# A two-layer decoder on one Trainium2 core: the gate norms of batches 0 and 1 tied to a place in VectorE's order

## The chip, the cores and the metric

The kernel runs on one core of a Trainium2 chip. The metric is the device time of one execution in microseconds (us), lower is better. Five engines work side by side, each through its own queue in order: TensorE (PE, with its weight loads shown as PEld), VectorE (DVE), ScalarE (ACT), GpSimd (POOL) and SyncE (SP), which issues most of the transfers (DMAs).

## What is computed

Six sublayers, each with a layer norm in front and a residual addition behind, act on `x` of 4 batches x 512 tokens x 256 channels, all in float32:

```python
x = x + _L0_attn_ref(_layernorm(x), ...)    # gated scan over time, 16 heads of 32
x = x + _L0_xattn_ref(_layernorm(x), ctx)   # cross attention, 16 heads of 16
x = x + _L0_ffn_ref(_layernorm(x), ...)     # 8 experts + 4 zero experts, top 2
x = x + _L1_attn_ref(_layernorm(x), ...)    # log-space recurrence
x = x + _L1_xattn_ref(_layernorm(x), ctx)   # ternary weights, int8 steps
x = x + _L1_ffn_ref(_layernorm(x), ...)     # 8 experts, top 2
```

The change lies where the second sublayer ends and the third begins. The third takes `layernorm(x)`, scores each token against 12 experts (`logits = x @ gate_w.T + bias`), takes the two best and mixes their outputs:

```python
logits = jnp.einsum('btd,ed->bte', x, gate_w) + expert_bias
topk_logits, topk_idx = jax.lax.top_k(logits, TOP_K)
topk_w = jax.nn.softmax(topk_logits, axis=-1)
```

## The kernel before

Layer 0's two mixers are one function, `l0_mixers`. Its core is a loop over 16 units `u` (and one more turn to end): unit `u` is batch `b = u // 4` and head group `m = u % 4`, four heads of the cross attention. A unit has eight steps `n`. Step `n` issues `exponents(u, ...)` (L919): PE multiplies keys by queries into a score tile of PSUM (two buffers), DVE takes the negated maxima into `tops` (L927), ACT takes the exponentials into `e` (L930). After it come the jobs that were appended with `after(n, job, ...)` for this step, in the order of appending.

In the steps of unit `u` the unit before is ended: `least(u - 1)` at step 1 finds the least maximum, `weigh(u - 1)` at step 2 forms the weights: PE spreads the value, DVE subtracts `tops` from it into `behind` (L950), ACT exponentiates it, POOL multiplies the values by it into `weighed` (L953). `gather_values(u - 1, j)` at steps 3 to 6 multiplies the weighted values by `e` on PE (L965, "av").

Other work is spread over the steps by hand: the first sublayer's work for later batches (`absorb`, `tokens` with the token norm, `turn_tokens`, `split` into q, `keep` and so on), `project` that adds the attention's output to `x` (L1060), `fold_piece` (products of the last sublayer's weights, from unit 11 on), and from unit 11 on the routing of the third sublayer by the class `Places`:

- `norm(b)` (L1497): a layer norm of a batch's four row tiles on DVE. `moments` (L173) issues four pairs of BATCH_NORM_STATS2 (L179) and BATCH_NORM_AGGREGATE (L180); `rstd` (L166) issues eleven small instructions one after another (L169, L160, then L162, L163, L164 three times); four TENSOR_SCALAR at L1504 write the normed tile `gh_b`. The small tiles of the norm have one buffer each.
- `transpose(b, c)` (L1508): PE turns four blocks of `gh_b` (L738), ACT copies them into `ght_b` (L1511), for the channel halves c = 0 and 1.
- `score(b, ...)` (L1513): 16 small matmuls and one DVE addition (L1523) give the logits; `pick` and `rank` find the two experts and the rows; `put` writes the rows by indirect transfers (L1575).

Two things set the order of the work. PE's instructions and the loads and stores on SP's queue are pinned in the order in which they are written (`pinned`, `turn` and `move` call `tc.keep_in_program_order`). The order on DVE, ACT and POOL is made when the kernel is built: what is written earlier comes first among what is ready by the planner's reckoning, so that an instruction whose inputs are there early may be put ahead of others that are written before it. `tc.add_manual_dep` with class `NoSync` adds an order between two instructions of one engine without a semaphore; the kernel uses it for `blank` and `put`, which are put behind the last `weighed` product on POOL.

The jobs of units 11 and 12 that the change concerns are these:

```python
if u == 11:
    after(1, g.norm, 0)
    for c in range(DC):
        after(4 + c, g.transpose, 0, c)
    after(5, g.norm, 1)
    after(6, g.score, 0, (0, 1))
elif u == 12:
    for c in range(DC):
        after(1 + c, g.transpose, 1, c)
    after(3, g.score, 1, (0, 1))
    after(4, g.pick, (0, 1))
```

Norms 2 and 3 follow in unit 13 and behind the loop.

Of the kernel before, what the change touches and what calls it, by code (L numbers as in the profile page):

```python
# [18 lines left out]
P = 128  # L19
# [4 lines left out]
QT = T // P  # L24
# [17 lines left out]
class Kernel:  # L42
# [127 lines left out]
        self.inverse_root(y, half, u)  # L170
        return y

    def moments(self, srcs, pool):  # L173

        nc, n = self.nc, len(srcs)
        st = pool.tile([P, n, nc.vector.BN_STATS_DIM], F32, tag="ln_st", name="ln_st")
        mv = pool.tile([P, n, nc.vector.BN_AGGR_DIM], F32, tag="ln_mv", name="ln_mv")
        for i, s in enumerate(srcs):
            nc.vector.bn_stats(st[:, i, :], s)  # L179
            nc.vector.bn_aggr(mv[:, i, :], st[:, i, :])  # L180
        return mv

# [358 lines left out]
def l0_mixers(k):  # L541
# [21 lines left out]
    with ExitStack() as es:  # L563
# [159 lines left out]


        normal, mixed, raw, sums_of, squares, factors, gated, outs = {}, {}, {}, {}, {}, {}, {}, {}
        weighing, near_of, factor_of = {}, {}, {}

        def normalize(b):
            normal[b] = k.layer_norm(b)
# [214 lines left out]
        def weigh(u):  # L944

            b, m = divmod(u, 4)
            ps, diag = lows[u]
            pinned(ps[:, P : P + 4], [(k.ones[:4, :], diag)])
            behind = sp.tile([P, QT, 4], F32, tag="behind", name=f"behind_{u}")
            nc.vector.tensor_sub(behind, ps[:, None, P : P + 4].to_broadcast([P, QT, 4]), k.tops[:, u])  # L950
            wt = weighed[u % 2]
            nc.scalar.activation(wt[:, :, :, 16], behind, AF.Exp)
            weighing[0] = nc.gpsimd.tensor_mul(  # L953
                wt[:, :, :, 0:16],
                vs[u],
                wt[:, :, :, 16:17].to_broadcast([P, QT, 4, 16]),
            )
# [232 lines left out]
        ps = bank("v_bias")  # L1190
# [25 lines left out]
        for u in range(units + 1):  # L1216
            b, m = divmod(u, 4)
            if m == 0 and b < NB:
                atts[b] = wk.tile([P, 4, T], F32, tag="att", name=f"att_{b}")

            then = {n: [] for n in range(8)}

            def after(n, f, *args):
                then[n].append((f, *args))

            if u + 1 < units:
                after(0, gather, u + 1)
                after(4, fetch_values, u + 1)
            if 0 < u < units:
                after(1, least, u - 1)  # L1230
                after(2, weigh, u - 1)
            if 2 <= u < 10:
                after(3, blank, u - 2)
            near_b, next_b, last_b = b + 1, b + 2, b + 3
            if u == FOLDING:

                mixers.close()
                k.fold_pool = ExitStack()
                k.fold_w = k.fold_pool.enter_context(tc.tile_pool(name="fold_w", bufs=2, side="right"))
                k.places = Places(  # L1240
                    k, k.fold_pool.enter_context(tc.tile_pool(name="places", bufs=1, side="right")),
                    move, bank, turn, pinned, new_ht,
                )
                after(7, fetch_fold, 0)
            elif u > FOLDING:
                if u < units:
                    for j, n in enumerate((0, 1, 2, 7)):
                        after(n, fold_piece, 4 * (u - FOLDING - 1) + j)
                g = k.places
                if u == 11:  # L1250
                    after(1, g.norm, 0)
                    for c in range(DC):
                        after(4 + c, g.transpose, 0, c)
                    after(5, g.norm, 1)
                    after(6, g.score, 0, (0, 1))
                elif u == 12:
                    for c in range(DC):
                        after(1 + c, g.transpose, 1, c)
                    after(3, g.score, 1, (0, 1))
                    after(4, g.pick, (0, 1))  # L1260
                    after(7, g.rank, (0, 1))
                elif u == 13:
                    for i in range(QT):
                        after(2 + i, project, 2, i)
                        after(3 + i, g.put, 0, i, weighing)
                    after(7, g.norm, 2)
                elif u == 14:
                    for c in range(DC):
                        after(1 + c, g.transpose, 2, c)
                    for i in range(QT):  # L1270
                        after(3 + i, g.put, 1, i, weighing)
                    after(3, g.score, 2, (2,))
                    after(3, g.pick, (2,))
                    after(6, g.rank, (2,))
                elif u == 15:
                    for i in range(QT):
                        after(3 + i, g.put, 2, i, weighing)
            if m == 0:
                if near_b < NB:
                    after(0, recall, near_b, 1)  # L1280
                    after(1, factor, near_b, 2)
                    after(3, recall, near_b, 2)
                    after(3, factor, near_b, 3)
                    after(5, recall, near_b, 3)
                    for j in range(3):
                        after(3 + 2 * j, emit, near_b, j)
            elif m == 1:
                if 1 <= b < NB - 1:
                    after(0, invert, b - 1)
                    after(2, give_back, b - 1)  # L1290
                    after(4, spread, b - 1, 0)
                    after(6, spread, b - 1, 1)
                if near_b < NB:
                    after(1, emit, near_b, 3)
                    after(2, absorb, near_b)
                    after(4, tokens, near_b)
                if next_b < NB:
                    for j in range(4):
                        after(2 + j, measure, next_b, j)
                    for j in range(4):  # L1300
                        after(4 + j, total, next_b, j)
            elif m == 2:
                if near_b < NB:
                    for c in range(DC):
                        after(1 + c, turn_tokens, near_b, c)
                    for mc in range(2):
                        after(3 + mc, split, near_b, mc, "q")
                        after(5 + mc, keep, near_b, mc, "q")
                if next_b < NB:
                    after(0, scale, next_b)  # L1310
                    after(2, scale_near, next_b)
                    after(4, scale_far, next_b)
                if last_b < NB:
                    after(5, normalize, last_b)
                if 1 <= b < NB - 1:
                    for i in range(QT):
                        after(4 + i, project, b - 1, i)
            elif next_b < NB:
                for j in range(4):
                    after(j, gated_values, next_b, j)  # L1320
                after(1, factor, next_b, 0)
                after(3, factor, next_b, 1)
                after(4, recall, next_b, 0)
                if last_b < NB:
                    for c in range(DC):
                        after(5 + c, mix, last_b, c)
            if u == units:
                after(0, least, u - 1)
                after(0, share_sums, NB - 1, 2)
                after(0, weigh, u - 1)  # L1330
                after(0, share, NB - 1, 2)
                for j in range(QT):
                    after(0, gather_values, u - 1, j)
                for m in range(2):
                    after(0, project_early, NB - 1, m)
            elif u > FOLDING - 1:

                done = divmod(u - 2, 4)
                after(0, share_sums, *done)
                after(1, share, *done)  # L1340
            if 0 < u < units:
                for j in range(QT):
                    after(3 + j, gather_values, u - 1, j)
                if m == 0 and b < NB - 1:
                    after(7, collect, b - 1)
            for n in range(8):
                if u < units:
                    exponents(u, n // 4, n % 4)
                for f, *args in then[n]:
                    f(*args)  # L1350
# [104 lines left out]
class Places:  # L1455
# [38 lines left out]
        self.carry = self.start  # L1494
        self.h, self.ht, self.logits, self.picks = {}, {}, {}, {}

    def norm(self, b):  # L1497
        k = self.k
        h = self.h[b] = self.pool.tile([P, QT, D], F32, name=f"gh_{b}")
        srcs = [k.x[:, t, :] for t in range(NT)[k.tiles(b)]]  # L1500
        mv = k.moments(srcs, self.pool)
        r = k.rstd(mv[:, :, 1], QT, self.pool)
        for i, s in enumerate(srcs):
            k.nc.vector.tensor_scalar(  # L1504
# [817 lines left out]
```

## Time and profile before

| | us |
|---|---|
| five runs: median (lowest to highest) | 1273.62 (1270.16 to 1276.92) |
| the profiled execution, its own time | 1269.21 |
| its span, first to last instruction | 1267.5 |
| PE busy | 998.0 (79%) |
| DVE busy | 812.1 (64%) |
| ACT busy | 412.6 (33%) |
| POOL busy | 188.8 (15%) |
| mean granted TensorE clock | 0.883 |

The profile is of one execution. Times in it count from its first instruction. In a timeline a line gives the start, the time taken, the engine, the source line, the operation, what is written and read, the shapes and the count (xN, neighbours of one kind are merged); in brackets stands the idle time before it and what ended it. In a table by stretches each engine has its busy time and the number of its instructions; PEclk is the granted clock of TensorE, 1.00 being full. The ends of matmuls are modelled, so neighbouring matmuls can overlap in the list.

### The profile page before, as it was taken

How to read it: one execution, taken by the hardware profiler on the slowest of the kernel's cores; microseconds unless marked ns; L12 is line 12 of the kernel's file. 1: busy time of each engine (PE TensorE's matmuls, PEld its weight loads, DVE VectorE, ACT ScalarE, POOL GpSimd, SP SyncE). 2: the span in 40 equal slices, each digit the busy share in tenths (PEclk: the TensorE clock that was granted, in tenths of full speed). 3: DMA queues.
4: the chain of work that ended last, by engine and by line, in shares of the span. 5: the costliest groups of instructions: out<-in, count | busy, mean ns of one | idle time of the engine just before them, and what ended most of it. 6: DMA issues, size and time to landing. Idle time of an engine off the chain costs nothing.

```text
span 1267.5 us, 12057 instructions
## 1 busy us (share of the span) xinstructions
PE 998.0 (79%) x3868; PEld 560.0 (44%) x3868; DVE 812.1 (64%) x1991; ACT 412.6 (33%) x708; POOL 188.8 (15%) x225
## 2 busy tenths in 40 slices
PE   5879588688876999789789999337754887779997
PEld 1444233233332566447566677114432443254443
DVE  6676697887679768534356931346776555986564
ACT  4513355455443454320111421022222443820000
POOL 5431112213113002222000000630012100000000
PEclk9989787888976999898799999668886998879999
DMA  5385515343433645535456261310010010020000
GB/s 155 101 267 203 145 49 162 108 136 127 135 119 110 208 132 182 165 108 180 151 183 185 90 225 45 104 50 0 1 38 1 33 51 17 1 67 0 32 19 20
DMA packets 90779, 129.97 MB, mean 103 GB/s; under 512 B 20268, under 2 KB 61740, under 8 KB 90700
## 3 DMA queue, kind: packets, MB, share of 16 engines
q1 hardware_dynamic: 84544, 111.29, 27.9%
q0 software_dynamic: 6144, 17.83, 4.1%
q8 instruction: 33, 0.54, 0.2%
q14 instruction: 38, 0.31, 0.1%
q10 hardware_dynamic: 20, 0.00, 0.0%
HBM read 86.56 MB, written 42.53 MB: 102 GB/s over the span
## 4 chain that ended last, share of the span: by engine, by line
PE 28%; DVE 13%; DMA 3%; ACT 2%; issue 2%; another core or an unknown queue 2%; ACTq 2%; POOL 0%; SPq 0%; POOLq 0%; DVEq 0%
PE y L212 9%; PE ef L212 7%; PE bav L212 2%; PE down L212 2%; DVE hid_tops L1868 2%; PE bsc L212 2%; ACTq L205 1%; PE f L212 1%; PE bet L2090 1%; PE bf L212 1%; PE gate L212 1%; DVE state L1790 1%; DMA W_f1T_sb<-in_W_f1T 1%; DVE q_tmp L1857 1%
## 5 line engine op out<-in xcount | busy, mean ns | idle before, releaser
L930 ACT ACTIVATE e<-score,tops 128x512 f32<-128x512 f32 x256 | 161.6, 686 | 171.7 <-DVE tops L927 100.5
L927 DVE TENSOR_REDUCE tops<-score 128x2 f32<-128x1024 f32 x128 | 155.7, 1218 | 47.2 <-PE score L588 43.1
L212 PE MATMUL y<-folded_sb,fht 128*128 128x512 f32 x256 | 112.8, 601 | 0.0
L588 PE MATMUL score<-query,key 64*128 64x512 f32 x256 | 68.0, 533 | 24.8 <-ACT e L930 19.7
L2178 DVE SCALAR_TENSOR_TENSOR x_sb<-y,tt_w,x_sb 128x256 f32<-128x256 f32 x128 | 61.8, 483 | 38.3 <-PE y L212 35.0
L965 PE MATMUL av<-e,weighed 128*32 128x512 f32 x512 | 76.6, 638 | 5.7 <-POOL weighed L953 5.7
L212 PE MATMUL ef<-sw,eact 128*128 128x256 f32 x320 | 79.1, 385 | 2.4 <-DVE ey L1668 2.4
L212 PE MATMUL ef<-eht,sw 128*128 128x320 f32 x256 | 78.4, 448 | 1.3 <-ACT eact L1657 1.3
L212 PEld LDWEIGHTS y<-folded_sb,fht 128*128 128x128 f32 x256 | 48.9, 193 | 59.9 <-issue 59.9
L588 PEld LDWEIGHTS score<-query,key 64*128 64x128 f32 x256 | 25.2, 197 | 100.7 <-ACT e L930 50.8
L588 PE MATMUL fold<-w_outT,w_in 128*128 128x256 f32 x256 | 66.1, 411 | 0.0
L212 PEld LDWEIGHTS ef<-sw,eact 128*128 128x128 f32 x320 | 58.5, 193 | 12.8 <-DVE ey L1668 5.1
L588 PE MATMUL o<-o_wT_sb,qk 128*128 128x256 f32 x128 | 46.9, 530 | 20.4 <-DVE qk L826 20.4
L212 PE MATMUL down<-W_downT_sb,state 128*128 128x256 f32 x96 | 33.7, 502 | 31.8 <-DVE state L1790 13.6
L212 PEld LDWEIGHTS ef<-eht,sw 128*128 128x128 f32 x256 | 48.6, 196 | 18.7 <-ACT eact L1657 2.0
L588 PEld LDWEIGHTS fold<-w_outT,w_in 128*128 128x128 f32 x256 | 50.5, 204 | 9.6 <-issue 2.6
L1657 ACT ACTIVATE eact<-ef 128x640 f32<-128x640 f32 x32 | 22.3, 703 | 98.2 <-PE ef L212 98.2
L212 PE MATMUL f<-aht,W_fT_sb 128*128 128x512 f32 x96 | 47.3, 652 | 6.4 <-issue 6.0
L588 PEld LDWEIGHTS o<-o_wT_sb,qk 128*128 128x128 f32 x128 | 32.8, 268 | 34.0 <-DVE qk L826 23.7
L203 PE MATMUL turn<-ident,h 128*128 128x128 f32 x96 | 17.1, 328 | 38.2 <-DVE ln_u L162 20.5
L1638 DVE COPY eht<-eturn 128x256 f32<-128x256 f32 x40 | 16.8, 420 | 43.7 <-PE eturn L1637 43.4
L1740 POOL DMA_INDIRECT got<-table,rows x32 | 30.8, 963 | 86.0 <-DVE neg_b L1732 76.6
(389 smaller groups left out, 1806.3 us busy)
## 6 DMA issues: line engine op xcount, KB each, us to landing
table<-zeros POOLq DMA_DIRECT2D x8, 1152.0 KB
factors<-far SPq DMA_DIRECT2D x64, 128.0 KB
key<-far_k SPq DMA_DIRECT2D x16, 512.0 KB
query<-far_q SPq DMA_DIRECT2D x16, 512.0 KB
w_in<-in_w_in SPq DMA_DIRECT2D x16, 512.0 KB
w_outT<-in_w_outT SPq DMA_DIRECT2D x16, 512.0 KB
rows<-table SPq DMA_DIRECT2D x8, 640.0 KB
table<-ey SPq DMA_DIRECT2D x8, 640.0 KB
```

Of the source, the lines that this page charges most:

```text
L203: nc.tensor.transpose(ps[:, i * P : (i + 1) * P], h[:, i, c * P : (c + 1) * P], self.ident)
L205: nc.scalar.copy(dst(c), ps)
L212: self.nc.tensor.matmul(out, lhs_t, rhs, start=(i == 0), stop=(i == len(pairs) - 1))
L588: nc.tensor.matmul(out, lhs_t, rhs, start=start and i == 0, stop=stop and i == len(pairs) - 1)
L927: nc.vector.tensor_reduce(top, ps, AX.X, ALU.max, negate=True)
L930: nc.scalar.activation(e[:, i, :], ps[:, i, :], AF.Exp, bias=top[:, i : i + 1])
L965: nc.tensor.matmul(avs[u][32 * h : 32 * h + 32, :], weighed[u % 2][:, j, h, :], es_of[u, h // 2, j][:, h % 2, :], start=(j == 0), stop=(j ...
L1638: nc.vector.tensor_copy(ht[:, :, i * P : (i + 1) * P], ps)
L1657: nc.scalar.activation(act[:, f, :].rearrange("p (j t) -> p j t", j=2), ps[:, :, :half], AF.Silu)
L1740: nc.gpsimd.indirect_dma_start(out=got[t, which], out_offset=None, in_=k.table, in_offset=bass.IndirectOffsetOnAxis(ap=k.rows[:, which, t ...
L1868: k.nc.vector.tensor_reduce(dst, src, AX.X, ALU.max, apply_absolute_value=True)
L2178: nc.vector.scalar_tensor_tensor(xt, ps[:, e, :], w[:, i, e4 + e : e4 + e + 1], xt, ALU.mult, ALU.add)
```

## The change

`moments` and `Places.norm` take an optional `behind`. Where it is given, each of the four BATCH_NORM_STATS2 gets a `NoSync` order behind the instruction that it holds. `weigh` keeps its DVE subtraction (`behind`, L950) in `weights[0]`. In unit 11 gate norms 0 and 1 are given `weights`: at both places it holds the subtraction of `weigh(10)`, which is issued in step 2 of unit 11. Norm 0 goes from step 1 to step 2, its two turns from steps 4 and 5 to 5 and 6, norm 1 from step 5 to 6 and the score of batch 0 from step 6 to 7. Everything else, norms 2 and 3 and the jobs of unit 12 too, is as it was.

```diff
-    def moments(self, srcs, pool):
+    def moments(self, srcs, pool, behind=None):
...
-            nc.vector.bn_stats(st[:, i, :], s)
+            stats = nc.vector.bn_stats(st[:, i, :], s)
+            if behind:
+                self.tc.add_manual_dep(
+                    stats.ins,
+                    behind[0].ins.name,
+                    mybir.DependencyInfo(mybir.DependencyClass.NoSync, mybir.DependencyReason.DATA),
+                    reason="behind a unit's weights",
+                )
             nc.vector.bn_aggr(mv[:, i, :], st[:, i, :])
...
-        weighing, near_of, factor_of = {}, {}, {}
+        weighing, weights, near_of, factor_of = {}, {}, {}, {}
...
-            nc.vector.tensor_sub(behind, ps[:, None, P : P + 4].to_broadcast([P, QT, 4]), k.tops[:, u])
+            weights[0] = nc.vector.tensor_sub(behind, ps[:, None, P : P + 4].to_broadcast([P, QT, 4]), k.tops[:, u])
...
                 if u == 11:
-                    after(1, g.norm, 0)
+                    after(2, g.norm, 0, weights)
                     for c in range(DC):
-                        after(4 + c, g.transpose, 0, c)
-                    after(5, g.norm, 1)
-                    after(6, g.score, 0, (0, 1))
+                        after(5 + c, g.transpose, 0, c)
+                    after(6, g.norm, 1, weights)
+                    after(7, g.score, 0, (0, 1))
...
-    def norm(self, b):
+    def norm(self, b, behind=None):
...
-        mv = k.moments(srcs, self.pool)
+        mv = k.moments(srcs, self.pool, behind)
```

## The prediction, made before the changed kernel was run

> **What bounds the kernel now.** I began with the page: PE is busy 79% of the span, DVE (VectorE) 64%, and the late part of the chain of waits lies behind the attention units, so a saving inside a unit counts only if it moves the unit's end. The 16 units are told apart in the list of DVE instructions by their eight "tops" reductions (L927). The first "tops" of units 9 to 13 start at 371.8, 393.6, 429.5, 450.9 and 472.5 us: unit 10 takes 35.9 us, unit 9 takes 21.8, unit 11 takes 21.4, unit 12 takes 21.6. Then the busy time by stretch, one row for each of units 10 and 11 (columns: length; PE, weight loads, DVE, ACT, POOL busy with counts; granted clock; DMA):
>
> ```profile
> core 0: us, PE busy (x) PEld busy (x) DVE busy (x) ACT busy (x) POOL busy (x), PEclk, DMA share, GB/s
> 393.60:429.50 35.90, 26.73 (x108) 13.72 (x108) 28.96 (x77) 13.08 (x22) 6.08 (x8) 0.72 0.40 127
> 429.50:450.90 21.40, 20.32 (x124) 12.95 (x125) 15.36 (x38) 11.56 (x21) 0.64 (x1) 1.00 0.44 141
> ```
>
> In unit 11 PE is the bound (20.32 of 21.40) and DVE has 6 us of air. Unit 10 is mixed, so I read its first 20 us in the timelines, DVE first:
>
> ```profile
> 401.93 2.20 DVE L190 TENSOR_SCALAR h<-x_sb,ln_mv,ln_y 128x256 f32<-128x256 f32 x4
> 404.05 0.68 DVE L164 SCALAR_TENSOR_TENSOR ln_y<-ln_u,ln_y 128x4 f32<-128x4 f32 x1
> 404.76 1.20 DVE L162 TENSOR_TENSOR ln_u<-ln_y 128x4 f32<-128x4 f32 x1
> ...
> 408.49 1.38 DVE L1504 TENSOR_SCALAR gh<-x_sb,ln_mv,ln_y 128x256 f32<-128x256 f32 x4
> 409.79 0.68 DVE L1036 TENSOR_TENSOR att<-att,share 128x512 f32<-128x512 f32 x1
> 410.39 1.21 DVE L927 TENSOR_REDUCE tops<-score 128x2 f32<-128x1024 f32 x1
> 411.52 0.16 DVE L950 TENSOR_TENSOR behind<-low,tops 128x16 f32<-128x16 f32 x1
> ```
>
> This is gate norm 0 (the L1504 rows write its "gh"). It is written in unit 11, step 1, but stands between the token norm of batch 3 ("h") and the third "tops" of unit 10. DVE has no gap over 0.1 us from 386.8 to 412.8. PE in the same stretch:
>
> ```profile
> 394.13 0.37 PE L937 MATMUL low<-ident,low 128*4 128x128 f32 x1
> 402.39 0.80 PE L738 MATMUL turn<-ident,h 128*128 128x128 f32 x2 [7.89 <-DVE h L190]
> ...
> 406.30 0.79 PE L588 MATMUL score<-query,key 64*128 64x512 f32 x2
> ...
> 409.30 3.78 PE L588 MATMUL q<-xht,w_q 128*128 128x512 f32 x4
> 413.85 1.07 PE L965 MATMUL av<-e,weighed 128*32 128x512 f32 x8 [0.77 <-POOL weighed L953]
> ```
>
> PE's order is pinned. It waits 7.89 us for "h", then works almost without a gap (0.26 us twice) until 413.1, at half clock (0.50 in the row 392.98 to 413.46), and waits 0.77 us for the weights. So gate norm 0's long tail at 404 to 410 delays the "tops", but PE is busy meanwhile: that is the point on which the forecast turns.
>
> **What is removed from units 9 and 10.** The undisturbed gate norm of the last batch runs from 571.40 to 576.75: 5.3 us (four L179/L180 pairs 1.75, eleven small steps at a pitch of 0.20 make 2.2, four L1504 1.4). Norm 0 costs more where it stands, since its L162 and L164 steps take up to 1.20 us while POOL runs two-input products (L1006): 5.7 us after "h", about 1.0 in front of "h" (one L179 at 400.57, L180s, L169, L160, L162, L163), 1.2 in unit 9 (L179 at 386.94, 390.04, 390.44): some 8 us of DVE.
> - Unit 9: its "tops" mostly start when their scores end (score 386.81 with 0.50, "tops" 387.55; 388.29 with 0.50, "tops" 388.83), so little follows. Step by step I get 0.2 at 387.55, 0.4 at 390.84, 0.5 at 393.55.
> - In front of "h": the token norm's own chain also needs 0.20 a step, and norm 0's steps sit in its waits. From 399.96 to 401.93 (1.97) it would still need about 1.7: 0.3 saved. So "h" is 0.8 us earlier and PE's whole train with it.
> - After "h": the third "tops" can follow its score (406.30 to 407.1, now 405.5 to 406.3) instead of 410.39, the weights are ready before q ends, and the wait of 0.77 goes. What is late next is PE itself: q waits for the turn's copy (ACT, 408.68), not for "tops". PE reaches "av" at 412.3 rather than 413.85; the clock row changes at 413.46, so the av train (1.0 us at full clock) runs 1.16 us at half and ends 413.9 instead of 414.85.
>
> Gain: **1.0 us**. Bounds: nothing, if "h" does not move; 7.7 at the other end, since unit 6, with the same token turn, q split and projection, lasts 28.2 us (first "tops" 292.6 to 320.8) against 35.9. I take 1.0 because the rows of PE give it. If the clock returns one period (3.4 us) sooner, at 410.04, q's second half and "av" run at full rate and the gain is 2.8.
>
> **What is added to unit 11.** Norm 0's first statistics now stand behind "behind" of unit 10, which ran at 437.29 to 437.38 on DVE; the wait itself costs no time, being an order on one engine. What is queued behind norm 0 is the "tops" of steps 3 and on, whose scores end near 438.6, 441.1 and 443.1. Norm 0's turns move from steps 4 and 5 to 5 and 6; the second of these rows is now where its first turn goes:
>
> ```profile
> 441.05 0.66 PE L738 MATMUL gturn<-ident,gh 128*128 128x128 f32 x4
> ...
> 443.07 0.66 PE L738 MATMUL gturn<-ident,gh 128*128 128x128 f32 x4
> 443.65 1.07 PE L965 MATMUL av<-e,weighed 128*32 128x512 f32 x8
> ```
>
> From 437.38 to 443.07 are 5.7 us. Norm 0 alone takes 5.3, and two "tops" at 1.14 come between: 7.6, less the last three "gh" (1.0), which the first turn doesn't need: the first turn is possible at 437.38+6.6=444.0, and the last "gh" at 445.0 lets the fourth turn end near 445.3 instead of 443.7. Loss: **1.4 us**, in a unit where PE has no air to take it back. Bounds: nothing, if one "tops" only comes between (5.3-1.0+1.1=5.4, under 5.7); 2.8, if norm 0 stands as a block before the "tops" of step 3, which then ends at 443.8, its exponentials (2 x 0.6) at 445.2, and the score of step 5 waits from 442.6 to 445.4.
>
> Norm 1 uses the same single buffers (ln_mv, ln_y), so it follows norm 0. Its statistics leave DVE's waits in unit 10 (419.70, 422.83, 426.19, each beside an L1060 addition while PE is busy), where they cost nothing, so nothing is gained. Behind norm 0 it needs 5.3 us by its turn at 455.7; before that, DVE's waits after 437.38 add to 6.6 us and 2.2 of norm 1 already lay there. 10.6 against 8.8 and the 1.4 of the stall: just fits, 0 to 0.5 us of loss, taken as 0. The score moves from step 6 to 7, the pick (462.85) and the first put (483.6) wait for batch 1 as before: nothing. No DMA is added; SP's and POOL's orders keep theirs, and the loads behind low_q (w_in at 419.93) move with PE.
>
> **Sum.** -1.0+1.4=+0.4 us. The profiled execution took 1269.21 us (span 1267.5 and 1.7 around it), so it would become 1269.6. That execution lies 4.4 us under the median of the five runs, 1273.62; on the median the sum gives **1274.0**. About 0.3%, 3.8 us, is what a measurement can tell from no change.
>
> **The clock, row and rule.** At 392.98 the clock fell to half although PE had been busy 1.94 us of the 3.42 before, and its longest wait there was 1.15 us. After 403.45 PE worked with 0.26 us of pause until it came back at 413.46. The Trainium skill, "TensorE: Matmul & The Clock Gate", section "Why this matters for your kernels", says that only idle gaps over about 3 us lose the clock: by it a stall of 1.4 us costs 1.4 and the sum stays +0.4; by the row it can cost half of each 3.4 us period that follows. The row speaks against the rule, so the next rival keeps its chance.
>
> **Rivals.**
> - **Slower: the turn stalls PE long enough to lose the clock.** Place: first "gturn" in unit 11. It decides once the stall passes about 1.4 us in one period (1.94 of 3.42 busy was too little at 392.98). Price: stall 2.5, then two to three periods at half, 1.7 each, in PE-bound work: 2.5+4.3-1.0=+5.8, so 1279.4. For it: PE without air in unit 11, and 7.6 us of DVE work for 5.7 us. Against: in 436.50 to 439.90 PE was busy 2.32 of 3.40 and kept the clock.
> - **Faster: unit 10 was DVE's.** If the early "tops" also let the exponentials and the clock come early, unit 10 falls to unit 6's 28.2: -7.7+1.4=-6.3, so 1267.3. For it: DVE without a gap for 26 us, ACT's wait of 12.3 us for "tops" in that unit. Against: PE's own train from 402.39 on.
> - **Nothing moves.** Only L179 is tied; if other work takes the freed places on DVE, "h" stays and the stall is small: 1273.6.
>
> **Chances.** Forecast 0.36 (range 1270 to 1277.4), slower rival 0.32, faster rival 0.25, nothing 0.07. Of the forecast's case 0.05 lies above +3.8 us, as the 2.8 bound plus one lost period shows: faster 0.25, same 0.38, slower 0.37. The range takes in both rivals: 1267 to 1281.
>
> **What would show it.** Right: no L1504 before "behind" of unit 10; third "tops" of unit 10 close behind its score; PE's wait for "h" near 7; a wait of PE for "gh" of 1 to 2 us in unit 11; unit 10 shorter by 1 to 3, unit 11 longer by 1 to 3. Wrong: unit 10 under 31 us (faster rival), a granted clock under 1.00 in unit 11 (slower rival), or later units or stages whose DVE order has changed, which I count at nothing.

## The result, and the profile after

The changed kernel takes 1275.82 us in the median (1264.23 to 1280.37, 50 runs), the kernel before 1270.75 us beside it on the same chips (1264.46 to 1280.08, 94 runs). The ratio is **1.0036, interval 1.0027 to 1.0045**: slower by 0.36%, about 4.6 us. Forecast was no change that can be measured (+0.4 us, 1274.0). That 1275.82 is only 1.8 us from 1274.0 is luck: the forecast was added to 1273.62, and the kernel before took 2.9 us less than that beside the changed one. The time also lies in the range, but the range took in both rivals; the change against the kernel before is on the side of the slower one. The profiled execution took 1276.98 us, with a span of 1275.3 us and a granted clock of 0.879 (before: 1269.21, 1267.5, 0.883).

From first "tops" to first "tops", units 9, 10, 11 and 12 took 21.8, 36.0, 21.3 and 21.6 us before. After they take 24.6, 32.1, 27.7 and 23.1. This is the table by stretches of the changed kernel, one row for each of these units, with the columns of the header line (length of the stretch first):

```profile
core 0: us, PE busy (x) PEld busy (x) DVE busy (x) ACT busy (x) POOL busy (x), PEclk, DMA share, GB/s
369.35:393.98 24.63, 14.89 (x67) 6.40 (x67) 20.71 (x56) 10.61 (x18) 4.69 (x6) 0.72 0.43 138
393.98:426.11 32.13, 26.62 (x106) 13.69 (x107) 18.32 (x42) 13.00 (x22) 6.07 (x7) 0.73 0.37 120
426.11:453.77 27.66, 22.80 (x124) 13.76 (x125) 20.93 (x65) 12.43 (x22) 0.64 (x1) 0.88 0.33 109
453.77:476.91 23.14, 22.32 (x128) 13.80 (x129) 15.08 (x38) 12.27 (x22) 0.64 (x1) 0.93 0.49 152
```

Read the DVE column first. In unit 10 DVE is 18.3 us busy where it was 29.0, so the norms have left it, and still the clock is 0.73 and PE works its 26.6 us. Units 9 and 10 must be taken together, because the first "tops" of unit 10 now stands behind the additions to `x` and marks its start later: 57.8 us (57.77) have become 56.8 (56.76), **1.0 us gained**. Then the granted clock of units 11 and 12: 1.00 in both before, now 0.88 and 0.93. Unit 11 has lost **6.3 us** and unit 12 **1.5 us**.

The gain is seen on PE in unit 10, beside the lines that the prediction shows of before:

```profile
397.70 0.37 PE L944 MATMUL low<-ident,low 128*4 128x128 f32 x1 [6.10 <-DVE low L942]
399.35 0.80 PE L745 MATMUL turn<-ident,h 128*128 128x128 f32 x2 [1.28 <-DVE h L197]
...
406.25 3.78 PE L595 MATMUL q<-xht,w_q 128*128 128x512 f32 x4
409.96 1.56 PE L972 MATMUL av<-e,weighed 128*32 128x512 f32 x8
```

Ahead of "turn" PE now waits twice, 6.10 us for the reduction "low" and 1.28 us for "h", 7.38 together, where before it had "low" at once and then waited 7.89 us for "h". Counted from the first "tops" of unit 9, "turn" starts after 30.00 us instead of 30.64. The wait of 0.77 us for the weights ahead of "av" is gone. From "turn" on PE works as before, at half clock until 411.01.

The loss begins on DVE, in the place where norm 0 now stands. The timeline of unit 11:

```profile
433.87 0.16 DVE L957 TENSOR_TENSOR behind<-low,tops 128x16 f32<-128x16 f32 x1
433.95 0.74 DVE L179 BATCH_NORM_STATS2 ln_st<-x_sb 128x6 f32<-128x256 f32 x2
...
435.48 1.19 DVE L934 TENSOR_REDUCE tops<-score 128x2 f32<-128x1024 f32 x1
...
436.87 0.42 DVE L179 BATCH_NORM_STATS2 ln_st<-x_sb 128x6 f32<-128x256 f32 x1
...
437.74 1.23 DVE L934 TENSOR_REDUCE tops<-score 128x2 f32<-128x1024 f32 x1 [0.38 <-PE score L595]
...
439.49 1.22 DVE L934 TENSOR_REDUCE tops<-score 128x2 f32<-128x1024 f32 x1
...
442.41 1.38 DVE L1511 TENSOR_SCALAR gh<-x_sb,ln_mv,ln_y 128x256 f32<-128x256 f32 x4
```

Norm 0 starts right behind "behind", as the change says. Between its steps stand three "tops" and four statistics of norm 1 (436.87, 438.94, 440.70, 441.10), so the first written tile is begun 8.4 us after "behind" has ended. PE, in the timeline of the same stretch, waits for it:

```profile
442.96 1.35 PE L745 MATMUL gturn<-ident,gh 128*128 128x128 f32 x4 [3.52 <-DVE gh L1511]
444.25 1.94 PE L972 MATMUL av<-e,weighed 128*32 128x512 f32 x8
446.11 0.79 PE L595 MATMUL score<-query,key 64*128 64x512 f32 x2
446.84 1.11 PE L745 MATMUL gturn<-ident,gh 128*128 128x128 f32 x4
```

The wait is 3.52 us; the two rows of "gturn" that the prediction shows of before have none. What follows takes nearly twice its time: eight "av" 1.94 us instead of 1.07. The granted clock was half from 441.73 to 448.56, and once more from 465.63 to 469.04 in unit 12, where PE waited for nothing longer than 0.63 us.

Behind the units the instructions of PE, DVE, ACT and POOL stand in the same order in both profiles. From the end of the last "tops" to the end they took 718.7 and 718.4 us in two executions of before and 722.0 after. Whether these 3.3 us belong to the change is open. On the faster chips of the experiments the kernels with both norms tied took 695.6 to 699.2 us in this stretch and two with none tied 699.0 and 706.0, which doesn't point to the tie; on the slower chip two more tied ones took 722.0 and 725.3 and one without these norms 717.5, which would allow it. A loss of 5 us is therefore read in the units, and whole times are read by ratio alone.

### The profile page after: what moved, and what is told of

Its sections match the earlier page's. It is cut to its first block, busy times and chain, and to the rows that moved or that the text cites. A ratio compares the mean times of both kernels' runs of the same rounds, so it can differ in the third digit from the quotient of the medians.

```text
span 1275.3 us, 12053 instructions
## 1 busy us (share of the span) xinstructions
PE 1003.7 (79%) x3868; PEld 562.3 (44%) x3868; DVE 810.4 (64%) x1991; ACT 412.4 (32%) x708; POOL 189.1 (15%) x225
## 5 line engine op out<-in xcount | busy, mean ns | idle before, releaser
L972 PE MATMUL av<-e,weighed 128*32 128x512 f32 x512 | 79.2, 659 | 5.0 <-POOL weighed L960 5.0
L595 PEld LDWEIGHTS o<-o_wT_sb,qk 128*128 128x128 f32 x128 | 31.6, 258 | 32.7 <-DVE qk L833 22.8
```

The costliest lines, as they stand in the source:

```text
L595: nc.tensor.matmul(out, lhs_t, rhs, start=start and i == 0, stop=stop and i == len(pairs) - 1)
L972: nc.tensor.matmul(avs[u][32 * h : 32 * h + 32, :], weighed[u % 2][:, j, h, :], es_of[u, h // 2, j][:, h % 2, :], start=(j == 0), stop=(j ...
```

## The experiments

The theory: PE's wait for the tied norm 0 is the loss, once by itself and once by the clock. Rivals: DVE's order in unit 10 should have brought more (the faster rival); norm 1 in between is the cause; the later steps cost by themselves; and, for unit 12, whether the clock fell there for the same reason. The kernels ran in four groups, each on another chip; on three of them the kernel before takes 1241 to 1243 us in the median, on the fourth (experiments 1 and 3 and the second filler of 4) 1271, so each ratio is against runs of before on the same chip. A trace of before itself on the fourth chip has 21.9, 36.0, 21.3 and 21.6 us for units 9 to 12, as in its first trace; the stages behind them were expected to take about 699 us there and took 718.4. Each row of a unit below is of one execution.

**1. The tie alone.** Norms 0 and 1 tied, turns and score at the steps of before:

```diff
-                        after(5 + c, g.transpose, 0, c)
-                    after(6, g.norm, 1, weights)
-                    after(7, g.score, 0, (0, 1))
+                        after(4 + c, g.transpose, 0, c)
+                    after(5, g.norm, 1, weights)
+                    after(6, g.score, 0, (0, 1))
```

> Both ties, but turns and score at the steps of the kernel before (turns of batch 0 at steps 4 and 5). PE then reaches the first gate turn a step sooner, and two tops instead of three stand ahead of gh on DVE. Theory (the turn waits for norm 0): a wait of about 4.1 us instead of 3.5, the clock lost as well, +4 to +6.5 us against the kernel before: the later step bought only half a us. Rival (the later step is what costs, since it pushes score and turns into the fold pieces of step 7): +2 us or less.

Ratio 1.0057 (1.0031 to 1.0084). PE's timeline has the longer wait:

```profile
443.13 1.36 PE L745 MATMUL gturn<-ident,gh 128*128 128x128 f32 x4 [4.12 <-DVE gh L1511]
```

The clock was half from 439.67 to 446.50 and from 466.98 to 470.39; units 9 to 12 took 24.5, 32.2, 27.2 and 23.2 us. The tie by itself makes the whole picture of the changed kernel, and a step less of room makes the wait longer.

**2. The steps alone.** The kernel before with the later steps and no tie (`after(2, g.norm, 0)`, turns at 5 and 6, `after(6, g.norm, 1)`, score at 7):

> The other half of the change by itself: norms 0 and 1, turns and score of batch 0 one step later, no order behind the weights. Theory (the tie makes the whole difference): norm 0's written tiles stand again before the third tops of unit 10, units 9 to 12 at 24.3, 36.0, 21.3 and 21.6 us to within 0.5 us, no wait for gh, ratio 1.000. Rival (the later turns and score cost by themselves, by delaying what follows them): unit 11 or 12 over 1 us longer, ratio 1.002 or more.

Ratio 0.9997 (0.9975 to 1.0019); units 9 to 12 took 21.9, 36.0, 21.4 and 21.6 us at full clock in 11 and 12 (the 24.3 us expected for unit 9 were a miss). On DVE norm 0 stands in unit 10 as before, ahead of "behind" of the unit's weights:

```profile
407.02 1.39 DVE L1504 TENSOR_SCALAR gh<-x_sb,ln_mv,ln_y 128x256 f32<-128x256 f32 x4
...
410.05 0.17 DVE L950 TENSOR_TENSOR behind<-low,tops 128x16 f32<-128x16 f32 x1
```

So the later steps neither cost nor move anything: where the norm is written does not place it, the tie does.

**3. No norms at all.** The kernel before without gate norms 0 and 1; the experts of batches 0 and 1 are routed by `x` itself:

```diff
     def norm(self, b):
         k = self.k
+        if b < 2:
+            self.h[b] = k.x[:, k.tiles(b), :]
+            return
```

> The kernel before without gate norms 0 and 1: their turns and puts read x itself, so the experts of batches 0 and 1 get rows that are not normalized. This takes 10.6 us of DVE work out of units 9 to 11. Theory (PE bounds both places, DVE's work there is nearly hidden): units 9 and 10 together are 1 us shorter, unit 11 as before, the whole -2 to -0.5 us. Rival (DVE bounds unit 10): units 9 and 10 fall by 6 us or more and the whole by 5 us or more.

Ratio 1.0015 (0.9989 to 1.0041); its experts get other rows, so the units are what is read here. The rows of units 9 and 10:

```profile
369.27:393.88 24.61, 14.98 (x67) 6.37 (x67) 20.72 (x57) 10.65 (x18) 4.69 (x6) 0.73 0.44 143
393.88:424.54 30.66, 25.15 (x106) 13.51 (x107) 18.28 (x43) 13.00 (x22) 6.06 (x7) 0.77 0.40 122
```

They are 55.3 us together, against 57.8 before. The clock came back one period earlier, at 407.82 where before has 413.46 (starts of unit 9: 369.3 and 371.8). With the norms gone altogether unit 10 does not fall to 28.2 us. The faster rival is refuted: DVE's 8 us of norm in units 9 and 10 lie nearly all beside PE's own work, and about 1 to 2.5 us is all that there is to gain.

**4. The wait filled, twice.** The changed kernel with matmuls that nobody uses ahead of the first gate turn, so that PE does not stand still:

```diff
+        def filler():
+            ps = bank("filler")[:, :D]
+            for _ in range(14):
+                pinned(ps, [(k.ident, k.x[:, 0, :])])
...
+                    after(5, filler)
                     for c in range(DC):
                         after(5 + c, g.transpose, 0, c)
```

> The changed kernel, with 14 matmuls (ident by 256 columns of x, result unused) put on PE just ahead of the first gate turn of unit 11, where PE waits 3.52 us for gh. They take 14 x 0.215 = 3.0 us at full clock, so they fit inside the wait. Theory (the stall also loses the clock): the granted clock stays 1.00 in units 11 and 12, the 2.8 us lost at half clock behind the stall goes (and 1.7 us in unit 12 perhaps), the wait itself stays near 3.5 us less the filler; against the kernel before +0.1 to +1.8 us. Rival (only the wait counts, the clock would fall anyway): +4 to +5 us as in the changed kernel.

Ratio 1.0041 (1.0021 to 1.0061). A product is two instructions, so 14 products took 6.31 us instead of the 3 meant, and unit 11 took 27.5 us: the size was a miss. The clock stayed 1.00 in unit 11 all the same. With 7 products:

> The first filler was twice too long: a product of this shape is two matmul instructions, 28 of them took 6.31 us, and the turn came at 446.69 instead of about 444. This one has 7 products, 14 instructions, 3.15 us at full clock, inside the wait of 3.5 us. Theory (the stall also loses the clock): the first gate turn starts where it did, no half clock between it and the end of unit 11, unit 11 lasts 25.0 us (27.7 less 2.7), and against the kernel before the time is +1 to +3 us. Rival (the lost clock costs nothing because DVE bounds unit 11 anyway): unit 11 stays at 27.5 us.

Ratio 1.0035 (1.0009 to 1.0061). PE's timeline, and then the rows of units 11 and 12 in the table by stretches:

```profile
440.72 3.29 PE L595 MATMUL filler<-x_sb,ident 128*128 128x256 f32 x14
444.31 1.20 PE L745 MATMUL gturn<-ident,gh 128*128 128x128 f32 x4 [0.30 <-DVE gh L1518]
```

```profile
427.44:453.05 25.61, 23.97 (x138) 15.69 (x139) 20.60 (x65) 12.55 (x22) 0.64 (x1) 1.00 0.39 126
453.05:474.66 21.61, 20.77 (x128) 13.61 (x129) 15.18 (x38) 12.14 (x22) 0.64 (x1) 1.00 0.51 153
```

The filler stands in the place of the wait (3.29+0.30 us for 3.52), the norm is as late, and unit 11 takes 25.6 us at full clock. This splits the 6.3 us of unit 11: 27.66-25.61=2.05 us are half clock, 25.61-21.34=4.27 us are the late norm (the wait, and 0.5 us more in the first turn, whose four blocks come one by one). The whole time, expected 1 to 3 us above before, shows no gain of this size over the changed kernel (4.4 us above, 1.1 to 7.8); with intervals of 0.5% it couldn't.

**5. Norm 1 out of the way.** The four statistics of norm 1 tied behind the last "gh" of norm 0 instead of behind the weights:

```diff
     def norm(self, b, behind=None):
         k = self.k
+        if b == 1:
+            behind = {0: self.last}
...
-            k.nc.vector.tensor_scalar(
+            self.last = k.nc.vector.tensor_scalar(
```

> The changed kernel, with the statistics of norm 1 tied behind the last instruction of norm 0, so that only tops stand between norm 0's steps. Theory (tops are most of what delays norm 0): the wait for gh falls only from 3.5 to about 2.7 us, the clock is still lost, +3.5 to +4.6 us against the kernel before. Rival (norm 1's four statistics are what delays norm 0): the wait falls to 2.1 us or less, the clock is kept, +1.5 us or less.

Ratio 1.0037 (1.0014 to 1.0060). The wait fell from 3.52 to 3.11 us:

```profile
445.18 1.36 PE L745 MATMUL gturn<-ident,gh 128*128 128x128 f32 x4 [3.11 <-DVE gh L1513]
```

The clock was half from 444.35 to 451.18. Unit 11 took 28.6 us and unit 12 22.0, 50.7 together where the changed kernel has 50.8; the first "tops" of unit 12 only comes later here, with five more PE instructions ahead of it. Norm 1's statistics were 0.4 us of the wait, no more. The rest is norm 0 itself and the three "tops" between its steps.

**6. Room for norm 0, from the other side.** The turns and the score go later: turns of batch 0 at unit 11, step 7 and unit 12, step 0, its score at step 1, batch 1's turns at 2 and 3, score at 4, pick at 5:

```diff
-                    for c in range(DC):
-                        after(5 + c, g.transpose, 0, c)
...
-                    after(7, g.score, 0, (0, 1))
+                    after(7, g.transpose, 0, 0)
                 elif u == 12:
+                    after(0, g.transpose, 0, 1)
+                    after(1, g.score, 0, (0, 1))
```

> The ties stay, but the turns of batch 0 move on to unit 11 step 7 and unit 12 step 0, its score to unit 12 step 1, the turns of batch 1 to steps 2 and 3, its score to 4, the pick to 5. Theory (the loss is PE's pinned turn waiting for norm 0): the wait for gh falls under 1.2 us, since a fold piece of 1.9 us stands ahead of the turn, the clock stays, unit 11 is near 22 us; against the kernel before -1.0 to +0.5 us. Rival (more DVE work behind the tie is the loss in itself, DVE bounds unit 11): unit 11 stays at 25 us or more and the kernel +3 us or more.

Ratio 1.0025 (1.0006 to 1.0043), 0.7 to 5.3 us above before where -1.0 to +0.5 was expected. The turn waits 0.51 us, unit 11 keeps the clock and takes 20.6 us, unit 12, which has its moved work, 25.0. But the chain behind it is later too, and PE meets it at the rank of the tokens at the end of unit 12:

```profile
472.09 0.43 PE L595 MATMUL ranks<-both,before 128*128 128x96 f32 x2 [1.72 <-DVE both L1540]
```

The clock was half from 473.94 to 480.77, unit 13 took 27.8 us instead of 24.7 (the figure of the other three kernels traced on this chip). The stall had moved. With the rank moved on too, from unit 12, step 7 to unit 13, step 0:

```diff
-                    after(7, g.rank, (0, 1))
                 elif u == 13:
+                    after(0, g.rank, (0, 1))
```

> As the late turns, but the rank of batches 0 and 1 goes from unit 12, step 7 to unit 13, step 0, so that PE's wait for it (1.72 us) has 3 us more of cover. Theory (a wait of over about 1.5 us on a PE-bound stretch costs itself and then 3.6 us of half clock): no wait over 1 us and full clock from unit 11 to unit 13, units 9 to 12 together 1.0 us shorter than before's 100.7 to 100.8 apart from what stands in unit 12, and units 9 to 13 together 0 to 1 us shorter than before's 127. Rival (the rank's wait only moves on with it): a wait for both of 1.5 us or more in unit 13 and units 9 to 13 some 3 us longer than before's. On the whole time the theory gives a ratio of 0.999 to 1.000, the rival 1.002 to 1.003.

Ratio 1.0009 (0.9989 to 1.0030). The waits are 0.50 us for "gh" and 0.55 us for "both". Units 9 to 13 took 24.5, 32.2, 20.6, 24.2 and 25.9 us, 127.3 together. Before's 126.9 and 127.1 are of the slower chip; on this one the kernel of experiment 2, with norm 0 where before has it, takes 125.5, so this one is 1.8 us longer and not, as expected, up to 1 us shorter. The clock was half from 458.09 to 461.50 in unit 12, without any wait near it. One such period costs at most 1.7 us, so about 1 us of the 2.8 is open. The drop is taken up in experiment 8.

**7. The norm a unit earlier.** Norm 0 tied behind the weights of unit 9 instead, issued in unit 10, step 3; norm 1 untied; turns and score as before:

```diff
                 after(7, fetch_fold, 0)
+                after(3, k.places.norm, 0, weights)
...
-                    after(2, g.norm, 0, weights)
                     for c in range(DC):
-                        after(5 + c, g.transpose, 0, c)
-                    after(6, g.norm, 1, weights)
-                    after(7, g.score, 0, (0, 1))
+                        after(4 + c, g.transpose, 0, c)
+                    after(5, g.norm, 1)
+                    after(6, g.score, 0, (0, 1))
```

> Norm 0 alone is tied, one unit earlier: it is issued in unit 10 step 3 behind the weights of unit 9, norm 1 and all turns and scores are as in the kernel before. DVE has 6 us of waits between 413.5 and 429.5 there, under a busy PE. Theory: the gain of about 1 us in units 9 and 10 is kept, nothing is lost in unit 11: -1.5 to -0.5 us against the kernel before. Rival (norm 0 behind the tie delays q's low half and the tops of unit 10 as much as it gave): -0.3 to +1.5 us.

Ratio 1.0018 (0.9996 to 1.0040). The rows of units 10 to 12 in the table by stretches:

```profile
397.02:429.21 32.19, 26.68 (x106) 13.69 (x107) 24.28 (x71) 12.99 (x22) 6.07 (x7) 0.73 0.36 112
429.21:450.52 21.31, 20.23 (x124) 12.89 (x125) 15.32 (x36) 11.48 (x21) 0.64 (x1) 1.00 0.46 151
450.52:472.14 21.62, 20.78 (x128) 13.62 (x129) 15.10 (x37) 12.80 (x24) 0.64 (x1) 1.00 0.53 165
```

This keeps the gain (24.6+32.2=56.8 us for units 9 and 10 against 57.8) and has no loss: units 11 and 12 are those of before. The whole time, expected 0.5 to 1.5 us under before, doesn't show it. Since norm 1 isn't tied here, it is an alternative as a whole, not a test of one norm. Run once more:

> Norm 0 issued in unit 10 behind the weights of unit 9, the turns and the score as before: the one form so far whose units 9 to 12 were shorter than before's (99.7 against 100.7). Theory (the 1.0 us is kept to the end): ratio 0.9992, that is 0.998 to 1.001. Rival (later stages give it back or more, as a first ratio of 1.0018 let one suspect): ratio 1.001 to 1.003 with units 9 to 12 again near 99.7.

Ratio 1.0006 (0.9985 to 1.0027); units 9 to 12 took 24.7, 30.7, 21.3 and 22.9 us, 99.5 together against 99.7 the first time and 100.7 before. It is made up differently: the clock came back a period earlier in unit 10 and was lost for one in unit 12. The gain of 1 us is seen in the units twice, and it is too small for the whole time: 1.0 of 1242 us is 0.08%, the intervals are 0.4% wide. No version is shown that beats the kernel before.

**8. What the drops in unit 12 are.** After norm 0's stall the clock fell again in unit 12 (465.63), but so it did where PE had not been stalled: without norms (459.02), with the long filler (466.76), with the late rank (458.09), in the second run of experiment 7 (459.83), though not in its first. PE was busy at least 3.40 of the 3.41 us of the period before each of these drops. The granted clock changes at multiples of 3.41 us, so I added up PE's work by such periods. Each of the periods ahead of these drops held all of a batch's score, or all but one of its 16 "gate" products of 12 columns, some 2 us. So 3.9 us more of such products were put in front of batch 0's score, in the kernel before:

```diff
+        def narrow():
+            ps = bank("narrow")[:, :12]
+            for _ in range(16):
+                pinned(ps, [(k.ident, k.x[:, 0, :12])])
...
+                    after(6, narrow)
                     after(6, g.score, 0, (0, 1))
```

> Before, with 16 more products of 12 columns on PE (written to a spare bank and used by nobody) ahead of the score of batch 0 in unit 11, step 6, about 3.9 us beside the score's own 2.0 us of 12-column products. It tests what the half clock in unit 12 of the changed kernel comes from. In all the traces the periods of 3.41 us after which the clock fell with PE busy throughout (before 458.1 to 470.4 us) held the whole score of a batch: wide products (128 columns and more) took 1.35 to 1.50 us of them, and 1.53 us or more in the periods that kept the clock. Theory (the clock counts how much of a period PE works on wide products; waiting and narrow products both count little): although PE never waits, the clock falls in unit 11 while or right after the narrow products run, for at least one period; unit 11 takes 21.3 plus 3.9 plus 1 to 3.4, that is 26.2 to 28.6 us. Rival (only waiting counts, the falls in unit 12 have another cause): full clock throughout unit 11, as with the 6.31 us of wide filler products, and unit 11 takes 25.2 us.

Ratio 1.0076 (1.0051 to 1.0101). PE's timeline, and the row of unit 11:

```profile
445.84 4.75 PE L588 MATMUL narrow<-x_sb,ident 128*128 128x12 f32 x32
450.44 3.57 PE L588 MATMUL gate<-gate_wT_sb,ght 128*128 128x12 f32 x16
453.94 1.94 PE L965 MATMUL av<-e,weighed 128*32 128x512 f32 x8
```

```profile
430.29:459.99 29.70, 28.62 (x156) 19.98 (x157) 15.33 (x37) 12.27 (x22) 0.64 (x1) 0.83 0.31 102
```

PE is busy from 441.38 on without a wait, and yet the clock falls at 448.35, 2.5 us into the narrow products, and comes back only at 458.59. The score, 1.96 us at full clock, takes 3.57. Unit 11 takes 29.7 us, over the 28.6 expected at most, since three periods were lost instead of two. 6.31 us of wide filler products in experiment 4 had kept the clock. Such narrow products thus count little for the clock, and the rival (only waiting counts) is refuted; whether it is their 12 columns or the weight load that each of them brings was not separated. This fits the drops in unit 12, but a score that lies wholly in one period isn't enough: the kernel before has one in unit 11 (all 16 products within 444.18 to 447.59) and keeps the clock. Counted from each product's start to the next one's, the products of 128 columns and more make 1.35 to 1.50 us of the periods ahead of the drops of unit 12, and 1.52 us or more of the periods with a score that kept the clock (1.53 in the one of before). How a score falls on the periods changes from run to run of one kernel, as the two runs of experiment 7 show. The 1.5 us of unit 12 in the profile after are therefore not shown to be the change's.

## Where the prediction was right and where it was wrong

**The gain was right.** Forecast -1.0 us in units 9 and 10, measured -1.0, and by the stated parts: "turn", which waits for "h", earlier by 0.6 us (0.8 reckoned), the wait of 0.77 us for the weights gone, the rest eaten by half clock. That the clock could return a period sooner (2.8 us) was left open in the text; it did so without norms and in one of the two runs of experiment 7, not in the changed kernel.

**The failed step is the size of the loss in unit 11**, the +1.4 us of the sum: the late norm measured 4.3 us, and the clock, which the sum put at nothing, 2.05 more. "Norm 0 alone takes 5.3, and two 'tops' at 1.14 come between" gave a first turn at 444.0, 6.6 us after "behind", and a loss of 1.4 us. It came 8.9 us after "behind" (434.03 to 442.96), with a wait of 3.52 us: three "tops" stood between, 1.1 us more, with 0.38 us of DVE's own waiting ahead of the second, and statistics of norm 1. I had reckoned with the turn where it would have to be, 5.7 us after "behind"; but a norm that is late lets the next "tops" in front of its remaining steps, which makes it later still.

**"Norm 1 follows norm 0" was wrong in part.** Only its aggregates waited for the shared tile; its four statistics slipped between norm 0's steps. Experiment 5 prices that at 0.4 us, where I took 0 to 0.5 at another place. (The sum there, 10.6 us against 8.8 and 1.4, doesn't "just fit": it is 0.4 us over.)

**The slower rival happened**, for its stated reason. The condition it names (a stall over about 1.4 us, a period with 1.94 of 3.42 us busy or less) was met: PE was busy 0.87 us of the 3.41 before 441.73. Its price was 2.5 for the stall and 4.3 for the clock; the filler gives 4.3 us for the late norm and 2.05 for the clock in unit 11. The sum, -1.0+6.3=+5.3 us, is close to the rival's +5.8 and to the 4.6 us (3.4 to 5.7) of the whole times. That the rival's sum fits is in part luck: its stall was 1.8 us too small and its clock 2.2 us too dear. The forecast fell since 1.4 us of stall lay just under the point from which the rival decides, so an error of 2 us in one DVE order turned the case.

**The faster rival** was refuted by experiment 3, and **nothing moves** by the profile after.

**Row and rule.** The Trainium skill, "TensorE: Matmul & The Clock Gate", section "Why this matters for your kernels", has PE-idle gaps over about 3 us as what to avoid against drops of the clock. In unit 11 the waits of 3.11, 3.52 and 4.12 us lost it and those of 0.30 to 1.08 us kept it, which agrees. But the clock fell at the end of a period, when these three waits had lasted 2.29, 2.29 and 0.66 us. A wait of 1.72 us in experiment 6 lost it as well (PE busy 1.86 us of the period), and narrow products lost it with no wait. The row was the better guide: what fits these units is how much wide work a period of 3.41 us holds. In units 9 to 13 of all fourteen traces, periods with up to 2.08 us of PE work and the rest idle lost the clock, 2.15 us and more kept it; with narrow products and no idle time for the rest, 1.50 us of wide work lost it and 1.52 us kept it. These are no limits that hold everywhere: in other stages of the traces of before and after, periods with 1.54 to 1.99 us of work kept the clock, and in unit 6 one with 2.17 (before) and one with 2.26 us (after) lost it.

## What to carry to other kernels

An order tied by hand puts work where DVE has other duties: count every instruction that can come between the tied chain's steps up to the time when its result is really ready, not up to the time when it is due. Where PE has no air, a wait near two fifths of a clock period (about 1.4 of 3.41 us here) is priced with the half clock behind it. Moving the reader later moved the stall to the next reader (experiment 6); the norm a unit earlier had no stall (experiment 7), though its 1 us is shown in the units only. Some 8 us of DVE work taken out of a stretch that PE sets were worth 1 us.

## What was not expected of the hardware

Narrow products lose the clock: after 32 instructions of 12 columns and with the score's 16 behind them it was half for 10.2 us (448.35 to 458.59) while PE waited for nothing.

The chips differ on the same kernel: 1241 to 1243 us in the median on three, 1271 on the fourth. In two profiled executions, of the kernel before on the fourth and of the one with the later steps on one of the three, unit 14 takes 31.6 and 26.4 us, and in the fourth sublayer the slower execution has idle times with "issue" as their end (PE 8.22 us, ACT 13.17, DVE 17.50, all within 812 to 831 us); the faster one has none there of over 1.1 us. What the engines waited for there wasn't tried.
